# A four-layer graph network on one core: a fixed order of the work on three engines in layer 2, earlier mask fetches, and a bias add moved from GpSimd to VectorE

## The chip, the core and the metric

The kernel runs on one core of a Trainium2 chip. A core has a tensor engine for matmuls (PE; its weight loads are shown as PEld), VectorE (DVE), ScalarE (ACT), GpSimd (POOL) and SyncE (SP), each with its own queue of instructions. SyncE here only issues DMAs, GpSimd issues others and does some arithmetic. The metric is the device time of one execution in microseconds (us), as the median of three runs.

## The reference, cut to what matters

The program takes x (2708 x 512), adj (2708 x 2708, ones with probability 0.012 and on the diagonal) and weights, and applies four layers. Each adds its result to its input and normalizes the rows. Layers 2 and 3 are the ones at hand:

```python
# layer 2
node_att = softmax(x @ node_w, axis=0)
h = x @ edge_w
e = where(adj > 0, h @ h.T, NEG_BIG)
output = adj * (node_att * softmax(e, axis=1)) @ (x @ weight) + bias
x = _layernorm(x + output)
# layer 3
query, key, value = x @ Wq + bq, x @ Wk + bk, x @ Wv + bv
a = query @ key.T * scale + adj + adj
x = _layernorm(x + softmax(a, axis=-1) @ value)
```

All of it is in 32-bit floats.

## The kernel before, in words

Layers 2 and 3 are both built by `softmax_layer`. The 2708 nodes are 22 blocks of up to 128, taken in 11 groups of two (`GROUPS`, `NG` = 11; the last group has 128 + 20 rows and is called `REMNANT`). One step handles one pair: the group `gi` of rows whose softmax is computed, and the group `g` of keys at place k of that row group's order. So a layer has 11 x 11 = 121 steps, and `step(t)` is called once for each, with `LAG` = `NG` + 2 = 13 further calls to drain.

One call of `step` holds four stages that belong to different pairs:

- Fetching (`fetch`, `fetch_weights`). On SyncE's queue: the block of adj that masks the scores (tile `a_score` in layer 2, three buffers; `a_cols` in layer 3), the tile `e` of the scores and, thirteen steps later, the block of adj by which the exponentials are multiplied (`a_cols`, four buffers).
- Scores of step t. In layer 2 the score matrix h h^T is symmetric. A pair with g >= gi is computed by PE (`score_products`, L1355, into the PSUM tile `ps_s`, of which there are two buffers that the transposes `ps_e` share). ScalarE copies the raw scores (`s_raw`, L1394), and GpSimd's queue stores them to `scores` in DRAM. A pair with g < gi is "turned": its scores are fetched from DRAM (L1299) and not computed again (`score_rows`). Either way `masked` makes them into masked scores in two instructions: ScalarE scales the mask block to 0 or NEG_BIG (L1841), and VectorE combines it with the scores (L1842). Then comes the running maximum (L1330).
- Exponentials of step t - 11 (`begin_exp`, L1464 on VectorE and L1465 on ScalarE, or L1474 on ScalarE for turned pairs), and one step later `end_exp`: sums (L1506), multiplication by adj (L1845) and the combinations T of the exponentials (L1516, two buffers of tag `T`).
- The sum over the values for step t - 13 (`one_sum`, L1559 on PE), with seven products in place of eight block products: the combinations T meet combinations S of the values.

At the end of a row group (`end`) the results leave PSUM through tile `c` (L1640). `finish2` adds them to the input rows r (L1875, r has been loaded by `load_rows`, L1862), and puts two pieces of work for each block on a list, of which one is taken per step: `norm` (normalize the rows, L117 to L126, transpose them on PE, L1211, and copy them to hT on ScalarE, L1212), and `project` (layer 3's values on PE, L131; a copy of them on ScalarE to a tile with tag `T`, L1887; its store to `v_d`, L1888; on GpSimd, the bias of layer 3 added to the rows, L1889; and their store to `x_d`, L1890). The rows are layer 3's residual input, and layer 3 loads them again by `load_rows`.

A scheduler decides the order of the instructions on each engine. It goes by the order in the program and by the time at which its own model holds an instruction for ready; then every engine runs its instructions in that order. `tc.issue_after(x)` binds it: what is traced inside, as far as it is on x's engine, is queued behind x. Before, layers 2 and 3 have no such bounds.

Of the kernel before, what the change touches and what calls it, by code (L numbers as in the profile page):

```python
# [29 lines left out]
def gnn_stack_kernel(  # L30
# [1195 lines left out]
            put(o, ps[:, :width])  # L1226

    def softmax_layer(
        att, psum, later, keys, vals, query, score, weigh, load_rest, finish, mirror, tile_a, lag
    ):  # L1230

        full, S, apart, vals4, po = vals
# [44 lines left out]
        def fetch(t):  # L1277

            gi, k = divmod(t, NG)
            if k == 0:  # L1280
                states[gi] = {
                    "gi": gi, "e": [], "a": [], "wa": {}, "t": {}, "mx": {}, "count": [0, 0],
                    "order": key_order(gi),
                }
            st = states[gi]
            g = st["order"][k]
            e = att.tile([P, GROUP, GW], F32, tag="e", name="e", bufs=lag + 3)
            st["e"].append(e)
            a = tile_a()
            st["a"].append(a)  # L1290
            if not turned(gi, g):
                load_a(a, gi, g)
                return
            i0, w = GSPAN[gi]
            j0 = GSPAN[g][0]
            for dst, src in rows_of(gi, a, adj[i0 : i0 + w, j0 : j0 + GW]):
                nc.sync.dma_start(dst, src)
            for dst, src in rows_of(gi, e, kept[g, gi]):
                nc.sync.dma_start(dst, src)  # L1299

        def fetch_weights(t):

# [34 lines left out]
        def score_rows(st, k):  # L1337

            gi, e, a = st["gi"], st["e"][k], st["a"][k]
            for x, y in by_rows(gi, e, a):  # L1340
                score(x, x, y)
            running_max(st, k, "rows")

        def score_products(st, k):
# [3 lines left out]
            e = st["e"][k]  # L1348
            ps = psum.tile([P, GROUP, GW], F32, tag="ps_s", name="ps_s")
            own = mirror and g == gi and g != REMNANT  # L1350

            def block(jb, i):
                j = BLOCKS[GROUPS[g][jb]][0]
# [104 lines left out]
        def begin_exp(st, k):  # L1458
            gi, g = st["gi"], st["order"][k]
            w = GSPAN[gi][1]  # L1460
            if not turned(gi, g):
                e = st["e"][k][:, :, :w]
                nm = st["nmax"][:, :w].unsqueeze(1).to_broadcast([P, GROUP, w])
                nc.vector.tensor_tensor(e, e, nm, ALU.add)  # L1464
                nc.scalar.activation(e, e, AF.Exp)  # L1465
                return
            m = st["count"][0]
            st["count"][0] += 1
            if m == 0:
                st["sums"] = small.tile([P, GROUP, NG], F32, tag="sums", name="sums", bufs=2)  # L1470
            for b, it in enumerate(GROUPS[gi]):
                n = BLOCKS[it][1]
                e = st["e"][k][:n, b, :]
                nc.scalar.activation(  # L1474
                    e, e, AF.Exp, bias=st["nm"][:n, b : b + 1],
                    accum_out=st["sums"][:n, b, m : m + 1],
                )

        def end_exp(st, k):
            gi, g = st["gi"], st["order"][k]  # L1480
            w = GSPAN[gi][1]
            e = st["e"][k]
            if turned(gi, g):
                ps = psum.tile([P, GROUP, GW], F32, tag="ps_s", name="ps_e")
                for jb in range(GROUP):
                    for b, it in enumerate(GROUPS[gi]):
                        n = BLOCKS[it][1]
                        nc.tensor.transpose(
                            ps[:, jb, b * P : b * P + n],
                            e[:n, b, jb * P : (jb + 1) * P],  # L1490
                            ident[:n, :n],
                        )
                weigh(e[:, :, :w], ps[:, :, :w], st["wa"].pop(k)[:, :, :w])
            else:
                acc = st.get("acc")
                if acc is None:
                    acc = st["acc"] = att.tile([P, GROUP, GW], F32, tag="acc", name="acc", bufs=1)
                    if g != REMNANT:
                        nc.vector.tensor_copy(acc[:, :, :w], e[:, :, :w])
                    else:  # L1500
                        nc.vector.tensor_copy(acc[:, 0, :w], e[:, 0, :w])
                        nc.vector.memset(acc[:, 1, :w], 0.0)
                        nc.vector.tensor_copy(acc[:REST, 1, :w], e[:REST, 1, :w])
                else:
                    for d, x in by_rows(g, acc, e):
                        nc.vector.tensor_tensor(d[..., :w], d[..., :w], x[..., :w], ALU.add)  # L1506
                if weigh:
                    weigh(e[:, :, :w], e[:, :, :w], st["wa"].pop(k)[:, :, :w])
            if g != REMNANT:
                t = att.tile([P, 2 * GROUP, P], F32, tag="T", name="T", bufs=2)  # L1510
                if gi == REMNANT:
                    d = t.rearrange("p q i -> p (q i)")[:, :w]
                    nc.vector.tensor_tensor(d, e[:, 1, :w], e[:, 0, :w], ALU.subtract)
                else:
                    q = e.rearrange("p j (i c) -> p (j i) c", c=P)
                    sub = lambda d, x, y: nc.vector.tensor_tensor(d, x, y, ALU.subtract)  # L1516
                    sub(t[:, 0:2, :], q[:, 1:4:2, :], q[:, 0:2, :])
                    sub(t[:, 2, :], q[:, 3, :], t[:, 0, :])
                    sub(t[:, 3, :], q[:, 2, :], t[:, 2, :])
                st["t"][k] = t  # L1520
            if k == NG - 1:
                row_sums(st)

        def row_sums(st):

# [95 lines left out]
        def end(st):  # L1621
# [27 lines left out]
                parts = [c[:, 0, :], c[:, 1, :]]  # L1649
            for b, it in enumerate(GROUPS[gi]):  # L1650
                n = BLOCKS[it][1]
                later.extend(finish(it, parts[b][:n], rs[:n, b : b + 1], r[:n, b, :]))

        states = {}
        total = NG * NG

        def sum_step(t):
            gi, k = divmod(t, NG)
# [9 lines left out]

        def step(t):

            for u in range(AHEAD) if t == 0 else ():
                fetch(u)
            if 0 <= t + AHEAD < total:
                fetch(t + AHEAD)
            if weigh and 0 <= t + AHEAD + 1 - lag < total:
                fetch_weights(t + AHEAD + 1 - lag)
            front = t + 2 - lag
            st, k = at(front)
            opens = k == 0
            if st and not opens:  # L1680
                begin_exp(st, k)
            before, kb = at(front - 1)
            if before:
# [24 lines left out]

# [75 lines left out]

    AHEAD = 1
    LAG = NG + 2
    with (
        tc.tile_pool(name="att", bufs=2) as att,  # L1790
# [47 lines left out]

        def masked(e, ps, a):

            nc.scalar.activation(a, a, AF.Identity, bias=neg_big[: a.shape[0]], scale=1.0e30)  # L1841
            nc.vector.scalar_tensor_tensor(e, a, NEG_BIG, ps, ALU.max, ALU.min)  # L1842

        def times_adj(d, e, a):
            nc.vector.tensor_tensor(d, e, a, ALU.mult)  # L1845
# [8 lines left out]
        def tile3():  # L1854
            return att.tile([P, GROUP, GW], F32, tag="a", name="a_cols", bufs=4)

        def load_rows(src):
            def load(gi):
                i0, w = GSPAN[gi]
                r = att.tile([P, GROUP, F], F32, tag="r", name="r", bufs=1)  # L1860
# [11 lines left out]
        def finish2(it, po, rs, y):  # L1872
# [10 lines left out]
            def project():  # L1883
                ps = psum.tile([P, F], F32, tag="tp", name="ps_v")
                project_rows(ps, hT[:, :, i0 : i0 + n], wv_sb, n)
                v = att.tile([P, F], F32, tag="T", name="v3", bufs=2)
                nc.scalar.copy(v[:n], ps[:n])  # L1887
                nc.gpsimd.dma_start(v3_d[i0 : i0 + n], v[:n])  # L1888
                nc.gpsimd.tensor_tensor(y, y, bv_sb[:n], ALU.add)  # L1889
                nc.gpsimd.dma_start(x3_d[i0 : i0 + n], y)  # L1890

            return [norm, project]
# [12 lines left out]
            True,  # L1905
            tile2,
            LAG,
        )

        mqk, queries = [], []  # L1910
# [23 lines left out]

            nc.vector.scalar_tensor_tensor(e, a, 2.0, ps, ALU.mult, ALU.add)  # L1935

        def finish3(it, po, rs, y):
            i0, n = BLOCKS[it]
            nc.vector.scalar_tensor_tensor(y, po, rs, y, ALU.mult, ALU.add)

# [142 lines left out]
```

## Time and profile before

| what | us |
|---|---|
| median of 3 runs (3193.25 to 3204.16) | 3195.55 |
| the profiled execution | 3196.62 |
| its span, from first to last instruction | 3194.8 |
| of it, layer 2 (first mask scaling's products to layer 3's first scores) | 704.3 |
| of it, layer 3 | 877 |

The span is what the profile covers; the 1.8 us around it are start and end. The profile's busy shares are averages over the whole program. The change touches only the last half, so the stretches 1613.7 to 2318 and 2318 to 3195 have to be read by themselves. Busy time of PE is modelled at its end, and waits are put down to the engine or the DMA that came last.

### The profile page before, as it was taken

How to read it: one execution, taken by the hardware profiler on the slowest of the kernel's cores; microseconds unless marked ns; L12 is line 12 of the kernel's file. 1: busy time of each engine (PE TensorE's matmuls, PEld its weight loads, DVE VectorE, ACT ScalarE, POOL GpSimd, SP SyncE). 2: the span in 40 equal slices, each digit the busy share in tenths (PEclk: the TensorE clock that was granted, in tenths of full speed). 3: DMA queues.
4: the chain of work that ended last, by engine and by line, in shares of the span. 5: the costliest groups of instructions: out<-in, count | busy, mean ns of one | idle time of the engine just before them, and what ended most of it. 6: DMA issues, size and time to landing. Idle time of an engine off the chain costs nothing.

```text
span 3194.8 us, 39584 instructions
## 1 busy us (share of the span) xinstructions
PE 3106.3 (97%) x15176; PEld 2354.7 (74%) x15176; DVE 2052.8 (64%) x3797; ACT 1349.8 (42%) x1615; POOL 206.5 (6%) x304
## 2 busy tenths in 40 slices
PE   8898999999999999999999999999999999999999
PEld 7898987444444446885578787777668888888886
DVE  7968975777686684444267667767644555555565
ACT  7898986477867552001133333434301111111111
POOL 1101100000000000000011111110110000000000
PEclk9999999999999999999999999999999999999999
DMA  7866865146455413541144444555431111111111
GB/s 278 297 224 229 294 229 195 48 156 236 171 175 191 171 62 100 141 127 41 44 150 142 139 142 148 154 176 172 132 101 36 51 51 49 49 52 50 49 44 34
DMA packets 203635, 425.81 MB, mean 133 GB/s; under 512 B 20798, under 2 KB 134562, under 8 KB 197622
## 3 DMA queue, kind: packets, MB, share of 16 engines
q1 hardware_dynamic: 179454, 319.92, 32.2%
q0 software_dynamic: 23552, 101.26, 8.5%
q10 hardware_dynamic: 440, 2.10, 0.3%
q8 instruction: 119, 1.95, 0.2%
q14 instruction: 70, 0.57, 0.1%
HBM read 325.88 MB, written 95.87 MB: 132 GB/s over the span
## 4 chain that ended last, share of the span: by engine, by line
PE 74%; DVE 8%; issue 7%; ACT 5%; DMA 4%; POOL 1%; SPq 0%; DVEq 0%; POOLq 0%; ACTq 0%
PE po L1559 18%; PE ps_s L1355 17%; PE po L456 10%; PE ps_nb L1169 7%; PE ps_wide L1219 5%; PE po L438 4%; PE ps_hid L131 2%; PE ps_sup L1747 2%; PE ps_mlp L805 2%; ACT t L406 2%; ACT t L415 2%; PE ps_dec L936 2%; DVE t L414 2%; PE ps_v L131 1%; DVE e L1845 1%
## 5 line engine op out<-in xcount | busy, mean ns | idle before, releaser
L414 DVE SCALAR_TENSOR_TENSOR t<-t,a 128x2708 f32<-128x2708 f32 (+1 forms) x152 | 450.3, 2975 | 175.0 <-ACT t L406 164.8
L438 PE MATMUL po<-xw,t 128*128 128x129 f32 (+2 forms) x3872 | 445.1, 282 | 39.9 <-ACT t L415 25.7
L438 PEld LDWEIGHTS po<-xw,t 128*128 128x128 f32 (+2 forms) x3872 | 437.3, 192 | 47.4 <-ACT t L415 38.9
L406 ACT ACTIVATE t<-f1b,f2h 128x1354 f32<-128x1354 f32 (+1 forms) x304 | 414.4, 1412 | 62.5 <-PE po L456 33.1
L415 ACT ACTIVATE t<-t 128x2708 f32<-128x2708 f32 (+1 forms) x152 | 371.2, 2452 | 81.8 <-DVE t L414 79.7
L1355 PE MATMUL ps_s<-q,hT 128*128 128x256 f32 (+1 forms) x1848 | 405.5, 372 | 0.0
L456 PE MATMUL po<-t,emb 128*128 128x452 f32 (+3 forms) x1056 | 397.7, 545 | 3.9 <-ACT t L415 3.7
L1559 PE MATMUL po<-sup,e 128*128 128x256 f32 (+1 forms) x1512 | 397.3, 384 | 3.0 <-DVE c L1640 2.1
L1355 PEld LDWEIGHTS ps_s<-q,hT 128*128 128x128 f32 x1848 | 339.2, 190 | 49.8 <-issue 6.0
L456 PEld LDWEIGHTS po<-t,emb 128*128 128x128 f32 (+1 forms) x1056 | 193.5, 190 | 201.2 <-issue 190.9
L1559 PEld LDWEIGHTS po<-sup,e 128*128 128x128 f32 (+1 forms) x1512 | 264.3, 185 | 59.0 <-issue 21.5
L1559 PE MATMUL po<-held,T 128*128 128x256 f32 x1200 | 294.5, 380 | 4.4 <-DVE T L1516 4.4
L1559 PEld LDWEIGHTS po<-held,T 128*128 128x128 f32 x1200 | 226.5, 190 | 37.8 <-DVE T L1516 6.4
L1935 DVE SCALAR_TENSOR_TENSOR e<-a_cols,ps_s 128x512 f32<-128x512 f32 (+1 forms) x121 | 79.7, 659 | 239.6 <-PE ps_s L1355 233.7
L1355 PE MATMUL ps_s<-hT 128*128 128x256 f32 (+2 forms) x968 | 213.9, 372 | 3.8 <-DVE e L1845 2.8
L1355 PEld LDWEIGHTS ps_s<-hT 128*128 128x128 f32 x968 | 174.2, 190 | 31.1 <-DVE e L1845 3.2
L1841 ACT ACTIVATE a_score<-a_score,neg_big 128x512 f32<-128x512 f32 (+2 forms) x131 | 88.9, 686 | 249.6 <-DMA a_score<-in_adjT_dram 104.0
L1169 PE MATMUL ps_nb<-hid_hi,at 128*128 128x512 f32 x484 | 185.5, 390 | 0.4 <-DVE at L1161 0.4
L1169 PE MATMUL ps_nb<-hid_lo,at 128*128 128x512 f32 x462 | 179.9, 389 | 0.0
L1465 ACT ACTIVATE e<-e 128x512 f32<-128x512 f32 (+1 forms) x187 | 113.5, 617 | 132.8 <-DVE e L1464 132.4
L1516 DVE TENSOR_TENSOR T<-e 128x256 f32<-128x256 f32 x200 | 84.0, 421 | 124.5 <-PE po L1559 101.7
L1927 ACT ACTIVATE q<-ps_wide,uq 128x256 f32<-128x256 f32 (+1 forms) x44 | 20.5, 465 | 338.6 <-PE ps_wide L1219 338.6
(275 smaller groups left out, 3951.5 us busy)
## 6 DMA issues: line engine op xcount, KB each, us to landing
a<-adj_d SPq DMA_DIRECT2D x108, 677.0 KB
a_cols<-in_adjT_dram SPq DMA_DIRECT2D x200, 256.0 KB
a<-in_adjT_dram SPq DMA_DIRECT2D x42, 677.0 KB
adj_d<-a POOLq DMA_DIRECT2D x42, 677.0 KB, 6.3
kept<-t POOLq DMA_DIRECT2D x20, 1354.0 KB, 7.2
t<-kept SPq DMA_DIRECT2D x20, 1354.0 KB
raw<-in_adjT_dram SPq DMA_DIRECT2D x105, 256.0 KB
a_score<-in_adjT_dram SPq DMA_DIRECT2D x55, 256.0 KB
```

The lines of the kernel that those rows point to most:

```text
L131: nc.tensor.matmul(ps[:n], xt[:, c, :n], w[:, c, :], start=(c == 0), stop=(c == C - 1))
L406: tanh = nc.scalar.activation(tv[:, k, :], f1b[k][:n, :w], AF.Tanh, bias=f2h[:n, jt, h : h + 1], scale=0.5,)
L414: step = nc.vector.scalar_tensor_tensor(tv, tv, GUARD, ab, ALU.add, ALU.mult)
L415: exp = nc.scalar.activation(tv, tv, AF.Exp, scale=0.5)
L438: nc.tensor.matmul(po[k][b][:m, s * DR : (s + 1) * DR], t[own : own + n, k, i0 : i0 + m], values[own : own + n, jt, HP * p + k, :], start= ...
L456: nc.tensor.matmul(po[HB * k + q][:, :qw], values[r : r + n, jt, h * P : (h + 1) * P], t[r : r + n, k, q0 : q0 + qw], start=(place == 0), ...
L1169: nc.tensor.matmul(pos[it][:n], at, half[:, jt, :], start=(jt == 0 and k == 0), stop=(jt == NT - 1),)
L1219: nc.tensor.matmul(ps[:, :width], w(c, o), xt(c), start=(c == 0), stop=(c == C - 1),)
L1355: nc.tensor.matmul(ps[:, jb, i:w], keys[:, c, j : j + P], st["q"][:, c, i:], start=(c == 0), stop=(c == C - 1),)
L1465: nc.scalar.activation(e, e, AF.Exp)
L1559: nc.tensor.matmul(po[bank][rows, half, :], lhsT, rhs, start=(k == 0 and half == 0) if first is None else first, stop=last, skip_group_che ...
L1841: nc.scalar.activation(a, a, AF.Identity, bias=neg_big[: a.shape[0]], scale=1.0e30)
```

## The change

It has four parts, the first three in layer 2 alone.

1. Mask blocks are fetched two steps ahead (`AHEAD` 1 to 2). The stored scores of turned pairs are still fetched one step ahead, by a function of their own. Layer 3's fetches stay one step ahead.
2. The scaling of the mask block is taken out of `masked` and traced at the start of the scores' stage (`stretch`). Four bounds fix its place and those of its neighbours: exponentials behind the scaling before them ("scale"); scalings and raw-score copies behind this step's exponential ("exp"); masks and maxima behind the last instruction of this step's `end_exp` ("formed"), the parts traced later by `rest` too.
3. The projected values go to the half of `c` whose contents have been used, in place of a new tile with tag `T`.
4. The bias of layer 3 is added to the rows where layer 3 loads them (`load_rows`, on VectorE), in place of GpSimd's add before the store.

```diff
+        def fetch_scores(t):
+            gi, k = divmod(t, NG)
...
+            e = att.tile([P, GROUP, GW], F32, tag="e", name="e", bufs=lag + 3)
+            st["e"].append(e)
+            if turned(gi, g):
+                for dst, src in rows_of(gi, e, kept[g, gi]):
+                    nc.sync.dma_start(dst, src)
...
             for x, y in by_rows(gi, e, a):
+                last["scale"] = stretch(y)
                 score(x, x, y)
...
+            if mirror:
+                last["scale"] = stretch(st["a"][k][:, :, :w])
...
+        ahead = AHEAD if mirror else 1
...
-            if 0 <= t + AHEAD < total:
-                fetch(t + AHEAD)
-            if weigh and 0 <= t + AHEAD + 1 - lag < total:
-                fetch_weights(t + AHEAD + 1 - lag)
+            if 0 <= t + ahead < total:
+                fetch(t + ahead)
+            for u in range(1) if t == 0 else ():
+                fetch_scores(u)
+            if 0 <= t + 1 < total:
+                fetch_scores(t + 1)
             front = t + 2 - lag
+            if weigh and 0 <= front < total:
+                fetch_weights(front)
+
+            def behind(*which):
+                stack = ExitStack()
+                for name in which if mirror else ():
+                    if name in last:
+                        stack.enter_context(tc.issue_after(last[name].ins))
+                return stack
+
             if st and not opens:
-                begin_exp(st, k)
+                with behind("scale"):
+                    last["exp"] = begin_exp(st, k)
             before, kb = at(front - 1)
             if before:
-                end_exp(before, kb)
+                last["formed"] = end_exp(before, kb)
...
-                if turned(now["gi"], g):
-                    score_rows(now, kn)
-                else:
-                    rest = score_products(now, kn)
+                with behind("exp", "formed"):
+                    if turned(now["gi"], g):
+                        score_rows(now, kn)
+                    else:
+                        rest = score_products(now, kn)
             early = opens and turned(st["gi"], st["order"][0])
             if early:
-                begin_exp(st, 0)
+                with behind("scale"):
+                    last["exp"] = begin_exp(st, 0)
...
             if rest:
-                rest()
+                with behind("formed"):
+                    rest()
             if opens:
                 spread(st)
                 if not early:
-                    begin_exp(st, 0)
+                    with behind("scale"):
+                        last["exp"] = begin_exp(st, 0)
...
-    AHEAD = 1
+    AHEAD = 2
...
         def masked(e, ps, a):
-            nc.scalar.activation(a, a, AF.Identity, bias=neg_big[: a.shape[0]], scale=1.0e30)
             nc.vector.scalar_tensor_tensor(e, a, NEG_BIG, ps, ALU.max, ALU.min)
+        def stretch(a):
+            return nc.scalar.activation(
+                a, a, AF.Identity, bias=neg_big[: a.shape[0]], scale=1.0e30
+            )
...
+                if bias is not None:
+                    for b, it in enumerate(GROUPS[gi]):
+                        x = r[: BLOCKS[it][1], b, :]
+                        nc.vector.tensor_tensor(x, x, bias[: x.shape[0]], ALU.add)
...
-                v = att.tile([P, F], F32, tag="T", name="v3", bufs=2)
                 nc.scalar.copy(v[:n], ps[:n])
                 nc.gpsimd.dma_start(v3_d[i0 : i0 + n], v[:n])
-                nc.gpsimd.tensor_tensor(y, y, bv_sb[:n], ALU.add)
                 nc.gpsimd.dma_start(x3_d[i0 : i0 + n], y)
...
-            load_rows(x3_d),
+            load_rows(x3_d, bv_sb),
```

The rest of the diff makes `end_exp`, `begin_exp` and `times_adj` return their last instruction, and passes `c[:, b, :]` to `finish2` as `v`.

More of the change, by code (lines that the diff above doesn't have):

```diff
@@ L1228, in softmax_layer @@
     def softmax_layer(
-        att, psum, later, keys, vals, query, score, weigh, load_rest, finish, mirror, tile_a, lag
+        att, psum, later, keys, vals, query, score, weigh, load_rest, finish, mirror, tile_a, lag,
+        stretch=None,
     ):
@@ L1286, in fetch @@
             g = st["order"][k]
-            e = att.tile([P, GROUP, GW], F32, tag="e", name="e", bufs=lag + 3)
-            st["e"].append(e)
             a = tile_a()
@@ L1297, in fetch @@
                 nc.sync.dma_start(dst, src)
-            for dst, src in rows_of(gi, e, kept[g, gi]):
-                nc.sync.dma_start(dst, src)
+        def fetch_scores(t):
+            gi, k = divmod(t, NG)
+            st = states[gi]
+            g = st["order"][k]
+            e = att.tile([P, GROUP, GW], F32, tag="e", name="e", bufs=lag + 3)
[3 more added lines that the diff above has]
+                    nc.sync.dma_start(dst, src)
         def fetch_weights(t):
@@ L1464, in begin_exp @@
                 nc.vector.tensor_tensor(e, e, nm, ALU.add)
-                nc.scalar.activation(e, e, AF.Exp)
-                return
+                return nc.scalar.activation(e, e, AF.Exp)
             m = st["count"][0]
@@ L1473, in begin_exp @@
                 e = st["e"][k][:n, b, :]
-                nc.scalar.activation(
+                done = nc.scalar.activation(
                     e, e, AF.Exp, bias=st["nm"][:n, b : b + 1],
@@ L1477, in begin_exp @@
                 )
+            return done
         def end_exp(st, k):
@@ L1492, in end_exp @@
                         )
-                weigh(e[:, :, :w], ps[:, :, :w], st["wa"].pop(k)[:, :, :w])
+                done = weigh(e[:, :, :w], ps[:, :, :w], st["wa"].pop(k)[:, :, :w])
             else:
@@ L1498, in end_exp @@
                     if g != REMNANT:
-                        nc.vector.tensor_copy(acc[:, :, :w], e[:, :, :w])
+                        done = nc.vector.tensor_copy(acc[:, :, :w], e[:, :, :w])
                     else:
@@ L1502, in end_exp @@
                         nc.vector.memset(acc[:, 1, :w], 0.0)
-                        nc.vector.tensor_copy(acc[:REST, 1, :w], e[:REST, 1, :w])
+                        done = nc.vector.tensor_copy(acc[:REST, 1, :w], e[:REST, 1, :w])
                 else:
                     for d, x in by_rows(g, acc, e):
-                        nc.vector.tensor_tensor(d[..., :w], d[..., :w], x[..., :w], ALU.add)
+                        done = nc.vector.tensor_tensor(d[..., :w], d[..., :w], x[..., :w], ALU.add)
                 if weigh:
-                    weigh(e[:, :, :w], e[:, :, :w], st["wa"].pop(k)[:, :, :w])
+                    done = weigh(e[:, :, :w], e[:, :, :w], st["wa"].pop(k)[:, :, :w])
             if g != REMNANT:
@@ L1512, in end_exp @@
                     d = t.rearrange("p q i -> p (q i)")[:, :w]
-                    nc.vector.tensor_tensor(d, e[:, 1, :w], e[:, 0, :w], ALU.subtract)
+                    done = nc.vector.tensor_tensor(d, e[:, 1, :w], e[:, 0, :w], ALU.subtract)
                 else:
@@ L1518, in end_exp @@
                     sub(t[:, 2, :], q[:, 3, :], t[:, 0, :])
-                    sub(t[:, 3, :], q[:, 2, :], t[:, 2, :])
+                    done = sub(t[:, 3, :], q[:, 2, :], t[:, 2, :])
                 st["t"][k] = t
@@ L1522, in end_exp @@
                 row_sums(st)
+            return done
         def row_sums(st):
@@ L1651, in end @@
                 n = BLOCKS[it][1]
-                later.extend(finish(it, parts[b][:n], rs[:n, b : b + 1], r[:n, b, :]))
-        states = {}
+                later.extend(finish(it, parts[b][:n], rs[:n, b : b + 1], r[:n, b, :], c[:, b, :]))
+        states, last = {}, {}
         total = NG * NG
+        ahead = AHEAD if mirror else 1
         def sum_step(t):
@@ L1669, in step @@
         def step(t):
-            for u in range(AHEAD) if t == 0 else ():
+            for u in range(ahead) if t == 0 else ():
                 fetch(u)
-            if 0 <= t + AHEAD < total:
-                fetch(t + AHEAD)
-            if weigh and 0 <= t + AHEAD + 1 - lag < total:
-                fetch_weights(t + AHEAD + 1 - lag)
-            front = t + 2 - lag
+            if 0 <= t + ahead < total:
[4 more added lines that the diff above has]
+                fetch_scores(t + 1)
+            front = t + 2 - lag
+            if weigh and 0 <= front < total:
[6 more added lines that the diff above has]
+                return stack
             st, k = at(front)
@@ L1839, in masked @@
         def masked(e, ps, a):
-            nc.scalar.activation(a, a, AF.Identity, bias=neg_big[: a.shape[0]], scale=1.0e30)
             nc.vector.scalar_tensor_tensor(e, a, NEG_BIG, ps, ALU.max, ALU.min)
+        def stretch(a):
+            return nc.scalar.activation(
+                a, a, AF.Identity, bias=neg_big[: a.shape[0]], scale=1.0e30
+            )
         def times_adj(d, e, a):
-            nc.vector.tensor_tensor(d, e, a, ALU.mult)
+            return nc.vector.tensor_tensor(d, e, a, ALU.mult)
         l2_only, l3_only = ExitStack(), ExitStack()
@@ L1855, in tile3, with load_rows @@
             return att.tile([P, GROUP, GW], F32, tag="a", name="a_cols", bufs=4)
-        def load_rows(src):
+        def load_rows(src, bias=None):
             def load(gi):
@@ L1867, in load, with finish2 @@
                     nc.sync.dma_start(r[:REST, 1, :], src[i0 + P : i0 + w])
+                if bias is not None:
+                    for b, it in enumerate(GROUPS[gi]):
+                        x = r[: BLOCKS[it][1], b, :]
+                        nc.vector.tensor_tensor(x, x, bias[: x.shape[0]], ALU.add)
                 return r
             return load
-        def finish2(it, po, rs, y):
+        def finish2(it, po, rs, y, v):
             i0, n = BLOCKS[it]
@@ L1907, in gnn_stack_kernel @@
             LAG,
+            stretch,
         )
@@ L1935, in biased, with finish3 @@
             nc.vector.scalar_tensor_tensor(e, a, 2.0, ps, ALU.mult, ALU.add)
-        def finish3(it, po, rs, y):
+        def finish3(it, po, rs, y, _):
             i0, n = BLOCKS[it]
```

## The prediction

> **What bounds the kernel now.** I read the busy shares first, then the same shares in the two stretches that the change can touch, then the tensor engine's own waits there, and last, one of these waits in order of time. The page's first part:
>
> ```profile
> PE 3106.3 (97%) x15176; PEld 2354.7 (74%) x15176; DVE 2052.8 (64%) x3797; ACT 1349.8 (42%) x1615; POOL 206.5 (6%) x304
> ```
>
> The windows view, for layer 2 (first mask scaling to layer 3's start) and layer 3:
>
> ```profile
> core 0: us, PE busy (x) PEld busy (x) DVE busy (x) ACT busy (x) POOL busy (x), PEclk, DMA share, GB/s
> 1613.70:2318.00 704.30, 687.38 (x3306) 550.38 (x3307) 492.45 (x1185) 275.25 (x599) 111.16 (x135) 1.00 0.51 152
> 2318.00:3195.00 877.00, 866.82 (x4286) 733.66 (x4284) 477.93 (x1124) 139.30 (x246) 22.56 (x38) 1.00 0.18 52
> ```
>
> The tensor engine is the bound in both, and the change neither adds nor drops a matmul. In layer 2 it stands idle for 704.30 - 687.38 = 16.9 us. That is the ceiling of what a better order can bring, about 0.5% of the whole. The waits view of PE in layer 2 names these idle times:
>
> ```profile
> PE ps_v L131 <- ACT hT L1212: 5.1, 4, 1.7
> PE po L1559 <- DVE T L1516: 4.4, 5, 2.0
> PE ps_s L1355 <- DVE e L1845: 2.8, 1, 2.8
> PE po L1559 <- DVE c L1640: 1.1, 2, 0.6
> ```
>
> The columns are total us, times, longest. The other six lines bring the sum to 16.6 us. The same view of ACT, DVE, POOL and SP says what held those engines up:
>
> ```profile
> ACT a_score L1841 <- DMA a_score<-in_adjT_dram: 104.0, 49, 5.9
> ACT a_score L1841 <- DMA a_score<-in_adj_dram: 90.2, 30, 8.2
> DVE T L1516 <- DMA v_d<-v: 18.2, 6, 7.2
> POOL r L1889 <- PE tp L1211: 136.3, 16, 38.0
> SPq L1862 <- DMA x_d<-r: 28.4, 9, 5.4
> ```
>
> ACT is idle most of the time, so 194 us of waiting for mask blocks cost nothing by themselves. They cost where something that PE needs stands behind them. The timeline shows one such place:
>
> ```profile
> 1803.87 0.66 DVE L1842 SCALAR_TENSOR_TENSOR e<-a_score,ps_s 128x512 f32<-128x512 f32 x1
> 1804.55 0.37 SPq L1297 DMA_DIRECT2D a_score<-in_adj_dram  x1
> 1809.47 0.72 ACT L1841 ACTIVATE a_score<-a_score,neg_big 128x512 f32<-128x512 f32 x1 [4.65 <-DMA a_score<-in_adj_dram]
> 1810.10 0.57 ACT L1212 COPY hT<-tp 128x512 f32<-128x512 f32 x1
> 1810.72 3.70 PE L131 MATMUL ps_v<-held,hT 128*128 128x512 f32 x8 [1.70 <-ACT hT L1212]
> ```
>
> The mask at 1803.87 frees a mask buffer, the fetch starts at 1804.55, the scaling at the head of ACT's queue waits 4.65 us for it. The copy of hT, whose transposes had ended at 1808.2, comes after it, and PE stands for 1.70.
>
> [...] Here a store of 256 KB by GpSimd's queue lands after 2.3 to 5.0 us (median 3.1), and the mask fetch above took 4.9. [...] beside the adds of L1889 one L1845 takes 2.56 us where its median is 0.68.
>
> **The change, part by part.** I sorted the 17 idle times of PE, as the timeline gives them, by their cause.
>
> 1. *Mask blocks two steps early, scalings in a fixed place.* Three waits for hT stand behind a scaling that waited for its block: 1.70, 1.16 and 1.58, 4.44 us. A step is 704.30 / 121 = 5.8 us. With AHEAD = 2 and three buffers a fetch can go out when the mask of three steps before is done, some 8 to 10 us before its scaling (two steps less an instruction or two), against 4 to 5 us to land. Its cost on SP is no new DMA, only another place: 121 fetches (0.37 us each) are moved past one step's a_cols, e and r loads. In the built order of the changed kernel hT's copy follows the square root directly at most of the group openings. I take all 4.44. Bounds: 0 if the fetch stays gated, 4.44.
>
> 2. *Values of layer 3 in c instead of T.* T has two buffers, and one of them held the projected values until their store landed. The waits 2.77 (at 1759.6), 0.73 (2030.4) and 0.38 (2260.1) end with a T released by v_d, 3.88 us. The values now lie in c, which is next written a whole group (about 60 us) later, against a store of some 3 us: no new wait. What is late next is the mask and ps_e behind it, which the engine has room for (DVE 70% busy). I take 3.88.
>
> 3. *No add on GpSimd.* The 22 adds (1.3 to 4.1 us each) leave POOL[...]. Of the 22, 16 stretched a VectorE instruction by 0.2 to 1.9 us, 14.6 us in sum (each against its line's median). Three idle times of PE end behind such a stretch: 0.97, 0.29 and, of 2.03, the 0.86 of the stretched mask: 2.12 us. The store of r no longer waits for PE's transposes and the add; r's next load, for which SP stood 28.4 us with mask and weight loads behind it, goes out some 2 to 9 us sooner. I count nothing more for that, since the gain in part 1 uses it.
>
> 4. *The bias in layer 3 on VectorE.* 21 adds of 128x512 and one of 20x512, each about 0.68 us as L1845 and L1506 take: 15 us on an engine that is 54% busy there (477.93 of 877). In the built order they follow the group's row sum (L1529), which came 7 to 10 us after the load's issue in nine of the groups. The last pair meets a load issued 1.1 us before that, but then VectorE had 5.40 us idle before its next T. Behind them wait the mask and ps_s's second buffer, one step of cover. I take 0; bounds 0 and 10 x 0.7 = 7 us if no cover were there.
>
> 5. *The fixed order itself* (masks behind the combinations of their step, scalings behind exponentials, exponentials behind the scaling before). No instruction is added. It is the one part whose price this trace does not show: below nothing it can remove some of the 4.99 us in the remaining waits, above it can build new ones. I take 0.4 us of loss; bounds -5 and +25 (rival C).
>
> The sum is 4.44 + 3.88 + 2.12 - 0.4 = 10.0 us. The profiled execution took 3196.62 us around a span of 3194.8, so it would take 3186.6. The median shown is 3195.55, 1.1 below it: forecast 3185.5.
>
> **The rivals.**
>
> *A, the rest goes too.* If the fixed order also clears the 4.99 us and the 1.17 left of the 2.03, nearly all 16.9 go[...]: 3195.55 - 17 = 3178.5. For it: the waits all lie at the group openings, where SP's queue stands. Against it: five of them (po behind c, the reciprocals, the first matmul behind sup) come from dependences that stay.
>
> *B, the waits only move.* The three mask buffers remain, and a fetch still waits for the mask of three steps before. SP waited 75.2 us in 35 fetches for exactly that (L1297 behind e L1842), so it was often at the fetch before its buffer was free; fetching earlier in the program then buys nothing. Left are 3.88 and part of 2.12, less new waits of 2 us: 3195.55 - 3 = 3192.5.
>
> *C, slower: one chain through ACT at the group openings.* A scaling now stands behind its step's exponentials. At an opening these wait for nm and nmax (ACT e L1474 waited 16.8 us in 5 times, the longest 10.9). Then the scaling is late, its mask is late, and the second ps_s buffer covers one step, 5.8 us. The longest case is 5.1 over that; at ten openings with half of it each, 2.5 x 10 = 25 us, less the 3.88 + 2.12 of parts 2 and 3: 3195.55 + 19 = 3214.6. It decides once an opening holds ACT longer than about 5.8 us. Against it: the built order keeps the first two exponentials and the nmax copy together, and ACT has 2.3 us of work per step.
>
> **How the numbers follow.** Forecast 0.50 (3181.5 to 3188.5), A 0.18, B 0.18, C 0.14. The bound between change and no change is 0.3%, 9.6 us. Of the forecast's half, 0.32 lies beyond it: faster 0.32 + 0.18 = 0.50. Within it are 0.18 of the forecast, B's 0.18 and 0.01 of C, where the chain costs little: 0.37. Slower is 0.13. The range leaves out A's far end below 3175, and C above 3201: 3175 to 3201.
>
> **What would show it.** PE's idle time in layer 2 near 7 us; ACT's waits for a_score's blocks down from 194 to under 60 us; no T behind a store of v; no line behind x_d's add, and SP's wait for r under 10 us; DVE's layer 3 busy time up by 15 us with PE's idle there unchanged. I am wrong if scalings wait for blocks as before (B), or if PE's idle time at the openings grows behind masks whose scaling came late (C).

## The result, and the profile after

The changed kernel takes 3177.6 us (median of 5 runs, 3173.6 to 3180.3) against 3193.3 of the kernel before beside it (5 runs): 15.7 us less. The ratio of the two is 0.9944, with a 95% interval of 0.9925 to 0.9962. It compares means, and one of the five runs before took 3204.2 us. A second series (e1 below) gave 3179.1, ratio 0.9955 (0.994 to 0.997).

The page's first part after, with busy time, share and instructions of each engine:

```profile
PE 3095.8 (98%) x15176; PEld 2349.5 (74%) x15176; DVE 2050.0 (65%) x3819; ACT 1347.0 (42%) x1615; POOL 163.5 (5%) x282
```

The windows view of the changed kernel, for layer 2 (here from its first score matmul to layer 3's first matmul) and layer 3. The columns are the stretch, its length, the busy time of PE, PEld, DVE, ACT and POOL, the granted clock, DMA share and GB/s:

```profile
1605.56:2287.81 682.25, 675.79 (x3274) 544.12 (x3275) 477.65 (x1179) 270.81 (x595) 70.55 (x114) 1.00 0.53 156
2287.81:3171.70 883.89, 873.70 (x4320) 739.82 (x4316) 490.19 (x1153) 140.76 (x249) 20.87 (x38) 1.00 0.19 52
```

The same stretches of the kernel before:

```profile
1614.34:2311.11 696.77, 680.49 (x3274) 544.29 (x3275) 489.35 (x1176) 273.25 (x595) 110.43 (x134) 1.00 0.51 152
2311.11:3194.84 883.73, 873.71 (x4320) 739.75 (x4316) 480.97 (x1132) 140.73 (x249) 23.28 (x39) 1.00 0.18 52
```

Layer 2 is 14.5 us shorter, layer 3 is as before. PE's idle time in layer 2 (length less busy) falls from 16.3 to 6.5 us, 9.8 us. The other 4.7 us come out of PE's busy time, with the same matmuls. By these numbers part of what a stall costs seems to be shown as busy; no run isolates it. The length of a stage is therefore the yardstick below, not the idle time in it. Layers 0 and 1, whose instructions are unchanged, began layer 2 at anything from 1605.3 to 1616.1 us in the fourteen profiles of this study. That is why medians of few executions are not taken as the price of a part. They serve as a check: in every run below, the change in layer 2's length lies inside the interval of the ratio of whole executions.

The six longest lines of the waits view of PE in layer 2 after (total us, times, longest):

```profile
PE po L1571 <- DVE e L1879: 2.8, 3, 1.1
PE po L1571 <- DVE c L1652: 1.8, 3, 0.9
PE ps_e L1499 <- DVE e L1879: 0.9, 1, 0.9
PE ps_s L1366 <- ACT sup L1784: 0.7, 1, 0.7
PE tp L1211 <- DVE r L126: 0.3, 1, 0.3
PE ps_v L131 <- ACT hT L1212: 0.2, 1, 0.2
```

The waits for hT went from 5.1 to 0.2 and those for T from 4.4 to nothing. On VectorE no T waits behind a store any more. The lines of ACT and, in the second fence, of SyncE's queue that the prediction named are these now (`...` stands for lines left out):

```profile
ACT a_score L1874 <- DMA a_score<-in_adj_dram: 94.2, 32, 6.6
ACT a_score L1874 <- DMA a_score<-in_adjT_dram: 87.1, 35, 6.6
```

```profile
SPq L1296 <- DVE e L1871: 95.0, 42, 8.6
...
SPq L1896 <- DMA x_d<-r: 11.9, 6, 3.5
```

Here is the surprise. ACT's waits for mask blocks were to fall from 194 to under 60 us and are 181. (The view puts further waits of the same scalings down to VectorE. With them it is 249 before and 194 after.) SyncE still waits for the mask's buffer (95.0 us; 75.2 before). The waits for hT went away, and yet the blocks come no earlier.

### The profile page after: what moved, and what is told of

It reads as the page before. It is cut to its first block, busy times and chain, and to the rows that moved or that the text cites. A ratio compares the mean times of both kernels' runs of the same rounds, so it can differ in the third digit from the quotient of the medians.

```text
span 3171.7 us, 39566 instructions
## 1 busy us (share of the span) xinstructions
PE 3095.8 (98%) x15176; PEld 2349.5 (74%) x15176; DVE 2050.0 (65%) x3819; ACT 1347.0 (42%) x1615; POOL 163.5 (5%) x282
## 4 chain that ended last, share of the span: by engine, by line
PE 77%; issue 11%; DVE 6%; ACT 3%; DMA 2%; POOL 1%; SPq 0%; POOLq 0%; DVEq 0%; ACTq 0%
PE po L1571 19%; PE ps_s L1366 18%; PE po L456 9%; PE ps_nb L1169 7%; PE po L438 7%; PE ps_wide L1219 4%; PE ps_sup L1777 2%; PE ps_mlp L805 2%; PE ps_hid L131 2%; DVE t L414 2%; PE ps_v L131 2%; PE ps_dec L936 2%; ACT t L406 1%; ACT t L415 1%; DMA kept<-t 1%
## 5 line engine op out<-in xcount | busy, mean ns | idle before, releaser
L1874 ACT ACTIVATE a_score<-a_score,neg_big 128x512 f32<-128x512 f32 (+3 forms) x131 | 88.6, 683 | 194.5 <-DMA a_score<-in_adj_dram 94.2
L1571 PE MATMUL po<-sup,T 128*128 128x256 f32 x480 | 142.5, 380 | 0.0
```

The lines of the kernel that those rows point to most:

```text
L1571: nc.tensor.matmul(po[bank][rows, half, :], lhsT, rhs, start=(k == 0 and half == 0) if first is None else first, stop=last, skip_group_che ...
L1874: return nc.scalar.activation(a, a, AF.Identity, bias=neg_big[: a.shape[0]], scale=1.0e30)
```

## The experiments

Two theories were set against each other. F is the prediction's part 1: the earlier fetch removes the waits for hT. O: three mask buffers gate the fetch whatever AHEAD is, and the fixed order of the instructions removed those waits. What the parts are worth was then asked from both ends: one part alone in the kernel before, or all but one in the changed kernel. The length of layer 2 and PE's idle time in it come from the one profile of each run, the median from all its executions (4 to 20), and the ratio is to the kernel before in the same series.

| run | kernel | layer 2, us | PE idle in it | median, us | ratio to before (95%) |
|---|---|---|---|---|---|
| before | | 696.8 | 16.3 | 3193.3 | |
| e5 | before once more | 697.4 | 14.8 | 3192.5 | 1.0006 (0.9996 to 1.0015) |
| after | | 682.3 | 6.5 | 3177.6 | 0.9944 (0.9925 to 0.9962) |
| e1 | after once more | 683.7 | 7.7 | 3179.1 | 0.9955 (0.994 to 0.997) |
| e2 | after, fetch one step ahead | 681.0 | 5.2 | 3178.1 | 0.9953 (0.9939 to 0.9968) |
| e3 | after, no fixed order | 684.1 | 7.7 | 3181.7 | 0.9963 (0.9949 to 0.9977) |
| e4 | before, fixed order alone | 688.8 | 11.1 | 3182.9 | 0.9971 (0.996 to 0.9981) |
| e6 | before, values in c alone | 684.9 | 7.5 | 3179.9 | 0.9958 (0.9943 to 0.9973) |
| e7 | before, bias moved alone | 689.6 | 12.2 | 3184.4 | 0.9979 (0.9969 to 0.9988) |
| e8 | before, values and bias | 683.2 | 6.4 | 3178.0 | 0.9952 (0.9937 to 0.9967) |
| e9 | e6, but T's turn still taken | 688.3 | 10.4 | 3184.4 | 0.9969 (0.9959 to 0.998) |
| e10 | after, values back in T | 686.5 | 9.4 | 3182.1 | 0.9966 (0.995 to 0.9982) |
| e11 | after, four mask buffers | 683.1 | 7.2 | 3180.5 | 0.9956 (0.994 to 0.9972) |
| e12 | before, three T buffers | 693.8 | 16.2 | 3187.5 | 0.9983 (0.9975 to 0.999) |

### The yardstick: both kernels once more (e1, e5)

No edit.

> The changed kernel once more, unaltered. Yardstick for all that follows is the length of layer 2, from its first score matmul to the first matmul of layer 3's scores: 696.8 us before, 682.3 after. If it is a property of the kernel, it comes back within 1 us, and layer 3 within 1 us of 883.9. Layers 0 and 1, whose instructions are the same, were 8.8 us shorter in the profile of the changed kernel: if that is chance, they lie anywhere from 1600 to 1618 us here, and the median difference of whole executions stays near layer 2's 14.5.

> The kernel before once more, unaltered. If the length of layer 2 is a property of the kernel, it lies within 1.5 us of 696.8 and layer 3 within 1 us of 883.7; layers 0 and 1 (1605 to 1616 us in the six profiles so far) may lie anywhere in that band. If layer 2 comes out below 692, the yardstick is too coarse for the parts and only medians of many runs can be used.

Measured: layer 2 at 683.7 and 697.4, 1.4 and 0.6 us from the first time, a little more than was said for e1. Layer 3 came within 0.2 us both times. So a difference of some 1.5 us in layer 2 is not told from chance. The means of the two profiles, 697.1 and 683.0, are used from here: the change is worth 14.1 us in layer 2. In e5 PE's busy time in layer 2 was 682.57 and its idle time 14.8, against 680.49 and 16.3 before, at nearly one length: the split between the two is softer than the length. Places inside the layer are softer too: the two profiles of before are 3.1 us apart at the end of the second row group (186.4 and 189.5 us into layer 2) and 0.3 us at the end of the tenth. The bound of 1.5 us rests on these two pairs alone.

### Does the earlier fetch do anything? (e2)

```diff
-    AHEAD = 2
+    AHEAD = 1
```

> The changed kernel with the mask blocks fetched one step ahead again; all else kept. Theory F (the prediction's part 1: the earlier fetch removes the waits for hT): layer 2 grows by 4.4 us to about 687, and PE's waits for hT return to some 5 us. Theory O (three mask buffers gate the fetch, and the fixed order removed the waits): layer 2 stays within 1.5 us of 682.3, ACT's waits for mask blocks stay near 181 us, PE's waits for hT stay under 1 us.

Measured: layer 2 at 681.0, no wait for hT in PE's list, ACT's waits for mask blocks 161.7 us. Theory F falls: beside the other parts, nothing is lost without the earlier fetch. Pairing the k-th fetch's issue with the k-th scaling in the trace shows why: the median distance was 3.3 us before, 3.4 in the changed kernel and 3.8 here, not the 8 to 10 of the prediction. With three buffers the fetch goes out when the mask of three blocks before lets its buffer go, and a place further ahead in the program cannot change that. The trace shows it fetch by fetch: 112 of 118 start within 0.1 us of the end of that mask in the changed kernel, and 103 of 118 did so already in the kernel before. Nor is it the transfer that fills the time. A block lies scaled in its buffer for 12.0 us at the median before, 10.1 after, until its mask has read it.

### What is the fixed order worth? (e3, e4)

e3, bounds off in the changed kernel; e4, the bounds alone (the changed kernel with the other three parts undone). In both, the scalings stay traced at the start of the scores' stage:

```diff
# e3
-                for name in which if mirror else ():
+                for name in ():
# e4
-    AHEAD = 2
+    AHEAD = 1
...
+                v = att.tile([P, F], F32, tag="T", name="v3", bufs=2)
                 nc.scalar.copy(v[:n], ps[:n])
                 nc.gpsimd.dma_start(v3_d[i0 : i0 + n], v[:n])
+                nc.gpsimd.tensor_tensor(y, y, bv_sb[:n], ALU.add)
...
-            load_rows(x3_d, bv_sb),
+            load_rows(x3_d),
```

> The changed kernel without the bounds of the fixed order (fetch two steps ahead, scalings traced first, values in c and bias on VectorE all kept). Theory O: about half of the gain of 14.5 goes back, layer 2 near 690, with waits for hT or T behind scalings, masks or exponentials in PE's list. Theory F: layer 2 stays within 1.5 us of 682.3. Rival C (the fixed order costs something, and the other parts earn more than they show): layer 2 falls below 680.

> The kernel before with the fixed order alone: fetch one step ahead, values of layer 3 in a tile with T's buffers, bias by GpSimd. Theory O: the order is worth about 8 us and values and bias about 6, so layer 2 is near 689, with T's waits for the store of the values (18 us on VectorE) still there. Theory F: near 697, as before. If values and bias alone are worth the whole, also near 697.

Measured: alone the order brings 8.3 us (688.8), as theory O said. But taken away from the changed kernel it costs 1.1 us (684.1), within chance, where O had said half the gain. So the order is able to remove these waits, and something else in the change removes them too. T's waits for the store, which were to stay at 18 us in e4, fell to 6.6.

Rival C, the chain through ACT, has one real place in e4. In its timeline the columns are start, duration, engine, line, operation, and in brackets the idle time before it and what ended it:

```profile
1757.39 0.72 ACT L1874 ACTIVATE a_score<-a_score,neg_big 128x512 f32<-128x512 f32 x1 [5.62 <-DMA a_score<-in_adjT_dram]
1758.01 0.61 ACT L1476 ACTIVATE e<-e 128x512 f32<-128x512 f32 x1
1758.53 0.35 ACT L1392 COPY e<-ps_parts 128x256 f32<-128x256 f32 x1
...
1758.94 0.70 PE L1400 MATMUL ps_s<-e,quarters 128*128 128x256 f32 x2 [2.27 <-ACT e L1392]
```

The exponential is bound behind the scaling, the scaling waits 5.62 us for its block, and PE pays 2.27 for the copy behind both. At the end of the fourth row group, 324.4 us into layer 2, e4 is where the kernel before was (324.1; 327.1 in e5). It gains its time later.

### Values and bias by themselves (e6, e7, e8)

```diff
# e6
-                later.extend(finish(it, parts[b][:n], rs[:n, b : b + 1], r[:n, b, :]))
+                later.extend(finish(it, parts[b][:n], rs[:n, b : b + 1], r[:n, b, :], c[:, b, :]))
...
-                v = att.tile([P, F], F32, tag="T", name="v3", bufs=2)
# e7
-                nc.gpsimd.tensor_tensor(y, y, bv_sb[:n], ALU.add)
...
+                if bias is not None:
+                    for b, it in enumerate(GROUPS[gi]):
+                        x = r[: BLOCKS[it][1], b, :]
+                        nc.vector.tensor_tensor(x, x, bias[: x.shape[0]], ALU.add)
# e8: both
```

> The kernel before with one part alone: the values of layer 3 in c in place of a tile with T's buffers. The prediction's part 2 gives 3.9 us: layer 2 near 693. If these waits were only taken over by the next late one, it stays within 1 us of 696.8. VectorE's waits for T behind the store (18 us before) go in either case.

> The kernel before with one part alone: the bias added on VectorE where layer 3 loads the rows, no add on GpSimd. The prediction's parts 3 and 4 give 2.1 us in layer 2 and nothing in layer 3: layer 2 near 694.6, layer 3 within 1 us of 883.7. A rival that makes the stretched VectorE instructions (14.6 us in sum) the main loss of the kernel before: layer 2 at 690 or below. VectorE is busy about 12 us less in layer 2 and 10 us more in layer 3.

> Both of these parts in the kernel before, and neither the fixed order nor the earlier fetch. The changed kernel without its bounds took 684.1, so parts 2 to 4 and the earlier trace of the scalings and the fetch together brought 12.6 us. If parts 2 to 4 are it: layer 2 at 684 to 687. By the prediction's sum (3.9 + 2.1): near 691. If the place where the scalings are traced matters more: above 691, near 693.

Measured: values alone 684.9, 12.2 us, where the prediction had 3.9; bias alone 689.6, 7.5 us, where it had 2.1; both 683.2, 13.9 us of the change's 14.1. These two small edits, without the fixed order and the earlier fetch, already give the changed kernel's time. (e3 is e8 with the earlier fetch and the scalings traced first; the two agree within 1.0 us.)

How can the values bring 12 us? Two things happen, at two places. For the first, the timeline of the kernel before, ahead of the longest of PE's waits:

```profile
1752.46 0.57 ACT L1887 COPY v<-ps_v 128x512 f32<-128x512 f32 x1
...
1753.32 0.54 POOL L1888 DMA_DIRECT2D v_d<-v  x1 [4.89 <-ACT e L1381]
...
1757.86 0.42 DVE L1516 TENSOR_TENSOR T<-e 128x256 f32<-128x256 f32 x1 [2.98 <-DMA v_d<-v]
1758.32 0.62 DVE L1516 TENSOR_TENSOR T<-e,T 128x128 f32<-128x128 f32 x2
1758.85 0.68 DVE L1845 TENSOR_TENSOR e<-ps_e,a_cols 128x512 f32<-128x512 f32 x1
...
1759.59 0.92 PE L1355 MATMUL ps_s<-hT 128*128 128x256 f32 x3 [2.77 <-DVE e L1845]
```

The store holds T's buffer until 1757.86, VectorE's queue stands behind it, the product L1845 that empties ps_e comes late, and PE has no PSUM tile for 2.77 us. This the prediction had counted. What it had not counted is the second thing, at a place where it saw no T at all. The kernel before, at its second wait for hT:

```profile
1945.81 0.60 PE L1211 MATMUL tp<-ident,r 128*128 128x128 f32 x4
...
1947.95 0.72 ACT L1841 ACTIVATE a_score<-a_score,neg_big 128x512 f32<-128x512 f32 x1 [1.87 <-DMA a_score<-in_adj_dram]
...
1948.58 0.57 ACT L1212 COPY hT<-tp 128x512 f32<-128x512 f32 x1
...
1949.20 1.13 PE L131 MATMUL ps_v<-held,hT 128*128 128x512 f32 x2 [1.16 <-ACT hT L1212]
```

The same place in e6:

```profile
1934.04 0.60 PE L1211 MATMUL tp<-ident,r 128*128 128x128 f32 x4
...
1934.67 0.59 ACT L1212 COPY hT<-tp 128x512 f32<-128x512 f32 x1 [3.29 <-PE tp L1211]
...
1935.67 1.02 PE L131 MATMUL ps_v<-held,hT 128*128 128x512 f32 x2
...
1937.29 0.72 ACT L1841 ACTIVATE a_score<-a_score,neg_big 128x512 f32<-128x512 f32 x1 [1.65 <-DMA a_score<-in_adj_dram]
```

The scaling waits for its block as before (1.65 us; 1.87). But the copy of hT now stands ahead of it on ACT's queue. No bound was put there: with the values out of T, the scheduler came to another order. Of the 20 copies of hT, 4 moved ahead of a scaling and 3 behind one. Of the waits for hT, 5.1 us before (3.7 in e5), 1.7 are left. The waits for T on VectorE, 35.8 us before with those behind the store and those behind PE (18.2 + 17.6), fall to 4.4:

```profile
DVE T L1516 <- PE po L1559: 17.6, 13, 4.9
```

```profile
DVE T L1516 <- PE po L1559: 4.4, 7, 0.8
```

The first line is from the kernel before, the second from e6, which has no other wait for T. How much each of the two things brings, e9 will bound.

The bias seems to work through VectorE's speed. VectorE's busy time in layer 2 falls by 12.2 us (489.35 to 477.19 in e7), near the 14.6 by which the prediction saw the adds stretch its instructions. In the kernel before, L126 takes 1.50 us beside an add (at 1880.58) where its median is 0.54, and the longest L1845 of the 66 that multiply e by a_cols takes 2.56 where the median is 0.68. The mean of these 66 falls from 730 ns to 675 in e7, and in the changed kernel, which has no such adds either, the longest takes 0.69 us. Why an add stretches its neighbours is not shown. Another order is hardly the cause: on ScalarE, at most 4 of layer 2's 575 instructions have another place than before, and no copy of hT is among them. But SyncE's wait for the rows r falls in the same run (28.4 to 12.0 us), and the two are not told apart. The wait of 2.77 shown above is 0.91 in e7, where T still stands behind the store, but for 1.62 in place of 2.98.

### Holding the buffer, or taking a turn of it? (e9, e12)

e9 is e6 with one column of the projection also copied to a tile of T's buffers, which nothing stores. The store leaves from c. e12 is the kernel before with three buffers for T and, for room, one fewer for e:

```diff
# e9: e6, and in place of v's tile
-                v = att.tile([P, F], F32, tag="T", name="v3", bufs=2)
+                t = att.tile([P, F], F32, tag="T", name="v3", bufs=2)
+                nc.scalar.copy(t[:n, :1], ps[:n, :1])
# e12, both places of the tag
-                t = att.tile([P, 2 * GROUP, P], F32, tag="T", name="T", bufs=2)
+                t = att.tile([P, 2 * GROUP, P], F32, tag="T", name="T", bufs=3)
...
-            e = att.tile([P, GROUP, GW], F32, tag="e", name="e", bufs=lag + 3)
+            e = att.tile([P, GROUP, GW], F32, tag="e", name="e", bufs=lag + 2)
```

> The kernel before with the values in c and stored from there (as in e6, layer 2 at 684.9), and yet a tile of T's two buffers taken for each block: one column of the projection is copied to it as well, and no store reads it. So T's buffers are still taken in turn 22 times, but held for one short copy and not until a store has landed. If the store's 3 us of holding is what cost (theory S): layer 2 stays within 2 us of 684.9. If a turn taken from T's two buffers costs by itself (theory R: ScalarE must wait until PE has done with one T, VectorE for ScalarE's copy, and one buffer is left for the next T): layer 2 near 693 or above, VectorE's waits for T behind PE's po at 15 us or more.

> The kernel before with a third buffer for T (for room, the score tiles e have one buffer fewer), the values still in T's buffers and the store still holding one of them. If the shortage of T's buffers is what the values cost: layer 2 at 684 to 687, VectorE's waits for T (35.8 us before) under 10. If it is the place of the values in ScalarE's and GpSimd's queues, or the missing e costs: 692 or above.

Measured: e9 at 688.3, between its two theories. All 20 copies of hT stand among the scalings as in the kernel before, so the 8.8 us that e9 gains come from the store no longer holding a T, without another place for these copies (some of VectorE's instructions do stand elsewhere). The other 3.4 of e6's 12.2 us are what the turn, its small copy and the old order cost together. They are lost late: at the end of the seventh row group e9 and e6 are level (505.6 and 505.9 us into layer 2), behind the place shown above, so the new order there brought no time that shows. VectorE's waits in layer 2 of e9 say what a turn does:

```profile
DVE T L1513 <- ACT v L1887: 6.5, 2, 5.2
DVE T L1516 <- ACT v L1887: 5.5, 2, 3.6
DVE T L1516 <- PE po L1559: 3.6, 6, 0.7
```

T now waits for ScalarE's small copy, 12.0 us in 4 times, and not for PE's sums, as theory R had it (3.6 us where 15 were forecast). One of the four, in e9's timeline:

```profile
2134.68 3.60 PE L131 MATMUL ps_v<-held,hT 128*128 128x512 f32 x8
...
2138.32 0.16 ACT L1887 COPY v<-ps_v 128x1 f32<-128x1 f32 x1 [5.26 <-PE ps_v L131]
...
2138.51 0.42 DVE L1516 TENSOR_TENSOR T<-e 128x256 f32<-128x256 f32 x1 [3.64 <-ACT v L1887]
```

The small copy itself waits for the projection on PE, 2.2 to 5.3 us at each of the four. Once a tile of T is promised to the values, the next T waits until PE has computed them. The waits for hT are 4.3 us (1.7 in e6), as the scalings are ahead again. How the 3.4 us divide between the two is not told apart.

e12 came out at 693.8, as the second of its forecasts said (692 or above). VectorE's waits for T (L1516) do fall, from 35.8 to 7.9 us (and 4.7 once for the last row group's T), as the first had it, and yet only 3.3 us are gained. At the end of the fourth row group e12 is level with e6 and e9 (320.7 us into layer 2; 321.0 and 320.1), and it loses behind that. Three things speak for why. The waits for hT are 6.2 us, the copies standing as before but for one. The scheduler put many other instructions of VectorE and SyncE in another order. And the missing buffer of e is felt: SyncE waits 33.9 us in 23 times for it (15.9 in 14 before), and the masks wait 29.4 us for stored scores (7.0 before). How much each takes is not told apart by this run.

### The marginal worth of the values in the changed kernel (e10)

```diff
+                v = att.tile([P, F], F32, tag="T", name="v3", bufs=2)
                 nc.scalar.copy(v[:n], ps[:n])
```

> The changed kernel with the values put back into a tile of T's buffers; fixed order, earlier fetch and bias on VectorE kept. If the parts add up (values 11.9 us, alone): layer 2 at 694. If they remove the same waits and overlap, as the runs so far say (order alone 8.0, values 11.9, bias 7.2, all 14): layer 2 at 684 to 688.

Measured: 686.5, as the overlap said. VectorE waits for T (L1527) for 28.2 us again (19.4 behind PE and 8.8 behind the store), not far from the 35.8 of before, and PE loses 3.5 us by it instead of 12. In the fixed order, it seems, less that PE needs stands behind a late T; no run here isolates that.

### Is it the mask buffers that gate? (e11)

```diff
-            count = 3 if name == "a_score" else 1
+            count = 4 if name == "a_score" else 1
...
-            e = att.tile([P, GROUP, GW], F32, tag="e", name="e", bufs=lag + 3)
+            e = att.tile([P, GROUP, GW], F32, tag="e", name="e", bufs=lag + 2)
```

> The changed kernel with four buffers for the mask blocks in place of three (for room, the score tiles e have one buffer fewer). The claim that the three buffers gate the earlier fetch: ACT's waits for mask blocks fall from 160 to 190 us to under 60, and SyncE's wait for the mask's buffer (95 us in 42 times) to under 50. As PE no longer waits behind these scalings, layer 2 stays at 680 to 684. If the blocks come late for another reason (SyncE's queue stands behind other waits, or the transfers are slow), ACT's waits stay above 120.

The waits views of ACT and, in the second fence, of SyncE's queue in layer 2 of e11:

```profile
ACT a_score L1874 <- DMA a_score<-in_adjT_dram: 81.0, 32, 7.0
ACT s_raw L1405 <- PE ps_s L1366: 80.9, 26, 9.4
...
ACT a_score L1874 <- DMA a_score<-in_adj_dram: 39.7, 18, 5.9
```

```profile
SPq L1296 <- DVE e L1871: 76.7, 39, 6.3
```

The fourth buffer takes ACT's waits for blocks to 120.7 us, and the distance from fetch to scaling, 3.4 us at the median and 6.2 at the upper quartile after, is 4.3 and 10.8. The forecasts of under 60, and of under 50 for SyncE (76.7), are missed. Even so it is the buffers that hold the fetches: 107 of 117 start within 0.1 us of the end of the mask of four blocks before. Layer 2 is at 683.1, unchanged. The second line shows why ACT's waits were a poor sign to begin with: its wait for PE's scores rises to 80.9 us from 42.8. ACT's waits in layer 2 add up to 418.6 us before, 409.7 after and 411.5 here. With only 271 us of work in the changed kernel's 682, ACT waits that long wherever its next operand is; only what stands behind the waiting instruction tells a cost.

## Why the prediction was right, and where it was not

**The forecast.** 10.0 us were predicted, and some 14 in layer 2 (15.7 between medians) came. That PE is the bound, that only its waits in layer 2 could go, and that layer 3 would not move were right: PE's idle time in layer 2 was forecast near 7 us and is 6.5. That the sum came near is in part luck, as the parts show. (The prediction speaks of 17 idle times of PE; the view holds 20, and its sums contain them all.)

**Part 1, the earlier fetch (4.44 us): this step failed.** "With AHEAD = 2 and three buffers a fetch can go out when the mask of three steps before is done, some 8 to 10 us before its scaling" was wrong: the distance is 3.4 us, and e2 shows the fetch to be worth nothing. The prediction's own rival B had named the reason (the three buffers remain), and the line that carries it, SyncE's wait for the mask's buffer, was in view. The waits for hT did go, but by another place of the copies on ACT's queue: 12 of 20 stand ahead of a scaling that they stood behind. The fixed order alone does it (e4: 0.7 us left), and the values in c in part (e6: 1.7 left).

**Part 2, values in c (3.88 us): the mechanism was right, the term mis-sized.** Alone it is 12.2 us. The sum held only the three waits of PE that end with a T released by the store. The 8.8 us of e9 come from the same cause, the store that holds a T, and are over twice the three waits: what a late T costs further down VectorE's queue, and what PE's busy time hides, was left out. So was the scheduler's new order, whose share is at most the other 3.4. With the fixed order in place it is 3.5 us, near the figure predicted, though by a different working.

**Part 3, no add on GpSimd (2.12 us): mis-sized.** Alone it is 7.5 us; with the values already in c, 1.7 (e6 to e8), hardly more than chance. The term held only the three idle times of PE that ended behind a stretched instruction. SyncE's wait for r fell from 28.4 to 11.9 us, just short of the "under 10" forecast, and to 12.0 in e7 from this part alone.

**Part 4, the bias in layer 3 (0 us): right.** L1905 takes 14.7 us in 22 instructions. VectorE's busy time in layer 3 rises by 9.2 us and not by the 15 of the forecast. (Part of the gap is known: the running maxima there take 1.7 us less, as two of them no longer stand beside an add of GpSimd's: 1.37 and 1.69 us before, against a median of 0.69.) PE's idle time there is 10.2 us against 10.0.

**Part 5, the fixed order (0.4 us of loss): wrong for the order alone, right beside the rest.** Alone it gains 8.3 us, outside the bound of 5 that was set. Beside the other parts it is worth 1.1 us, not told from nothing. Rival C's chain exists (2.27 us in e4), and the wait that would feed it, the exponentials' for nm, rose from 16.8 to 42.7 us. It did not reach PE in the changed kernel.

**The sum itself.** The three parts alone add up to 8.3 + 12.2 + 7.5 = 28.0 us and together give 14.1. They do not add, since each removes much the same stalls. The prediction's sum was nearer than its terms, as terms too small were added up as if they were separate. It also took idle time for the ceiling: of the 14.5 us between the first two profiles, 4.7 stood in PE's busy time. Rival A's time, 3178.5, came closer than the forecast, but not by its way: 6.5 us of idle time are left.

No run beat the changed kernel by more than chance: e2, without the earlier fetch, and e8, with values and bias alone, have its time.

## What to carry to other kernels

When several waits lie around one place, don't price an edit by the waits that name its buffer: try each edit alone and each left out, for waits that share a queue can be removed together, by any of several edits (here 28.0 us by three edits alone, 14.1 together). Where a scheduler places the instructions, a buffer is also an input to the order: moving one tile to another tag put copies ahead of waiting instructions, on another engine (4 of 20 in e6). And a fetch that was placed earlier in the program gained nothing while its buffer came free at the same time (layer 2 at 682.3 us with it, 681.0 without): before the edit, compare the fetch's start with the end of the instruction that frees its buffer.

## What was not expected

A buffer that a DMA leaves from can be dear beyond the waits that name it: the store of 256 KB (3.2 us from issue to landing at the median before) held one of two T buffers, which cost 8.8 us of layer 2 by e9, where the prediction counted 3.88. Even a tile that no store reads cost up to 3.4 us, by tying VectorE's queue to PE's projection and by the scheduler's order that comes with it. VectorE waited for T 35.8 us before and 28.2 in e10, and the price in layer 2 was 12.2 and 3.5 us: much the same wait, with other instructions behind it.
